# A fused transformer block: sums of four key tiles on GpSimd, and a last attention unit in which VectorE shares the adding and prepares the projection in pieces

## The chip, the cores and the metric

The kernel runs on one core of a Trainium2 chip. The metric is the time of one execution in device microseconds (us), the median over several runs. The core has five engines that run their own instruction streams and wait for each other by semaphores: TensorE (PE in the profile; PEld is its loading of weights), VectorE (DVE), ScalarE (ACT), GpSimd (POOL) and SyncE (SP), which here only issues DMAs. All arithmetic is in 32-bit floats.

## The reference, cut to what matters

The reference is a conditioned transformer block on x of shape (2, 2048, 512): two batches of 2048 tokens with 512 features.

```
mod = silu(cond) @ Wada + bada                     # six vectors of 512 for each batch
xm  = layernorm(x) * (1 + sc_a) + sh_a
q, k, v = xm @ Wqkv                                # 16 heads of 32 features
attn = softmax(where(causal, q k^T / sqrt(32), -inf))
x = x + gt_a * ((attn v) @ Wproj + bproj)          # "projection" below
xm = layernorm(x) * (1 + sc_m) + sh_m
x = x + gt_m * (gelu(xm @ W1 + b1) @ W2 + b2)      # the MLP, 2048 wide
```

The softmax needs, for each query and head, the sum over all keys of the exponentials. This row sum is what the change is about, together with the division by it.

## The kernel before, in words

The kernel goes through batch 0 (QKV, attention, projection), batch 1 (the same), and then the MLP for both.

**Units.** The 16 heads are taken in four groups `c` of four heads, since four heads of 32 features fill 128 partitions. The queries are taken in four blocks `i` of `QB` = 512. A pair (c, i) is a unit; there are 16 for each batch, in the order (0, 1, 2, 3) of `i` for c = 0 and (0, 2, 1, 3) for the others, so the last unit is (3, 3). The last four units' blocks are `last_order` = 0, 2, 1, 3, and the projection takes the blocks in this order.

**Steps.** A unit goes through the key tiles of 128 that a causal query block can see: `4 i` full tiles, and then three steps at the diagonal (the four partly masked tiles, two of which share a step). Unit (c, 3) has 12 full steps and 3 at the diagonal. In each step `scores_t` does for four heads: TensorE puts minus the row maximum into a PSUM bank (`st<-fold,sel`), adds the transposed scores (`st<-qst,kst`), and ScalarE takes the exponential into an SBUF tile (`e<-st`). At the diagonal GpSimd sets the masked part of `e` to zero (`affine_select`). There are four `st` banks and `E_BUFS` = 12 tiles `e`, three steps' worth.

**Maxima.** The row maximum of a unit has to be known before its steps. So while one unit is in its steps, TensorE computes score tiles of later units (`s<-kst,qst`, in PSUM banks of the pool `ps_s` or in borrowed `st` banks) and VectorE reduces them (`mx<-s`, or `junk<-s,causal` for the diagonal tiles). `due` spreads these tiles over the steps, by fixed costs, up to `AHEAD` = 2 units ahead. In the last unit nothing is left to do ahead.

**Values and row sums.** `LAG` = 2 steps later TensorE multiplies `e` by the values (`o<-e,vv`) and by ones, for the row sums (`sm<-…,ones`). Both have 32 output rows for each head. At the diagonal each step has its own row sums (`sm<-e,ones`). For the full key tiles GpSimd first adds the `e` of two steps (`pair_sums`, `ee<-e`, into one of `EE_BUFS` = 6 tiles), and one group of matmuls (`sm<-ee,ones`) serves the two. Work that comes later waits in a list `pending` with the step at which it is issued; `flush` issues it after that step's scores.

```
ee = pair_sums(even, es)                  # line 663
pending.append((now + LAG + 1,            # line 664
    lambda f=row_sums, ee=ee, first=n_step == 1: f(ee, first, False)))
```

**End of a unit.** `finish` copies `o` and `sm` to SBUF and writes them to HBM: attention outputs `od` and row sums `sd`. They are divided only at the projection. `inverses` loads the sums of a block as a [128, 64] tile `r`, VectorE takes the reciprocal, a DMA writes it to HBM (`rd`), and four DMAs, one for each `c`, read it back, each value broadcast over the 32 rows of its head, into a tile `rb` of 1 MB. Then VectorE multiplies the attention output by `rb`.

**The last unit and the projection.** At step 3 of the last unit `prefetch` (line 341) loads what the projection needs first, into the free key buffer `kst0`: Wproj, the outputs of the first two blocks (`at_s`), and x; it also takes the inverses of these two blocks and multiplies by them, as one VectorE operation of 128x2048 for each block (line 373). At step 7 `gate_weights` (line 375) brings the gate row into PSUM and multiplies bproj (`bgate`) and Wproj by it. `project_phase` (line 849) then takes 16 tiles of 128 tokens: GpSimd adds `bgate` to x (line 880), TensorE multiplies, VectorE adds the two, takes the statistics of the next layernorm and SP writes the row out. The inverses of the third and fourth blocks are taken there, in tiles n = 0 and n = 3, with their DMAs on ScalarE's queue (line 873). Between the tiles come the layernorm and transposes of the next stage.

**Order.** A scheduler orders instructions on each engine by its own model of the time, within what the data allow. Matmuls, the exponentials and the copies of `finish` are kept in program order (`mm`, `act`); other VectorE and GpSimd operations and the DMAs are placed by the scheduler. So VectorE's products with `rb` may be placed earlier or later than where they are written. All matmuls have line 190 in the profile, since one helper issues them.

Of the kernel before, what the change touches and what calls it, by code (L numbers as in the profile page):

```python
# [8 lines left out]
F32 = mybir.dt.float32  # L9
# [18 lines left out]
def dit_block_kernel(  # L28
# [31 lines left out]

    nc = tc.nc
    B, T, D = x.shape
    HID = W1.shape[1]
# [7 lines left out]
    NG = T // MT  # L73
    LAG = 2
    E_BUFS = 12
    EE_BUFS = 6
    AHEAD = 2

    const = ctx.enter_context(tc.tile_pool(name="const", bufs=1))
# [192 lines left out]
    class Row:  # L272
# [31 lines left out]
        def load_queries(self, u):  # L304
# [8 lines left out]
                )  # L313
            self.qst[u] = t

        def inverses(self, i, rb, queue):

            sums, inv = [
                d[self.b][i].rearrange("c h (p q) -> (c h p) q", p=P // (C * HC))
                for d in (sd, rd)
            ]
# [15 lines left out]
        def prefetch(self):  # L341

            st = bp.tile([P, HC, T], F32R, tag="kst0", name="kst")
            st = st.bitcast(F32).rearrange("p h t -> p (h t)")
            self.at_s = [  # L350
                st[:, n * C * QB : (n + 1) * C * QB].rearrange("p (c q) -> p c q", c=C)
                for n in range(2)
            ]
            self.xt_s = [st[:, (2 * C + n) * QB : (2 * C + n + 1) * QB] for n in range(TQ)]
            self.wproj = st[:, 3 * C * QB :].rearrange("p (c d) -> p c d", c=C)
            t = self.old_queries()
            self.next_s = [t[:, n, :] for n in range(TQ)]
# [12 lines left out]
            for k in range(2):  # L370
                rb = self.old_queries()
                self.inverses(last_order[k], rb, nc.sync)
                nc.vector.tensor_tensor(self.at_s[k], self.at_s[k], rb, ALU.mult)
# [107 lines left out]
    def attention_phase(row):  # L481
        b, vv, kst, qst = row.b, row.vv, row.kst, row.qst
        with pool(f"att{b}") as ap, pool(
# [4 lines left out]
            def scores_t(u, step, n):  # L488

                def st_bank():
                    return ps_stp.tile([P, QB], F32, tag="st", name="st")

                c, i = units[u]  # L500
                tiles = steps_of[u][step]
                q0 = tiles[0][1]
                w = sum(QB - q for _, q in tiles)
                sts, es = [], []
                row.score(max(0, n - 5))
                n = min(n, 5)
                for h in range(HC):
                    g = slice(h * HD, (h + 1) * HD)
                    st = st_bank()
                    mm(  # L510
                        st[:, :w], sel[g, :], fold[u % 2][g, q0 : q0 + w],
                        start=True, stop=False,
                    )
                    sts.append(st)
                for h in range(HC):
                    at = 0
                    for j, q in tiles:
                        mm(
                            sts[h][:, at : at + QB - q],
                            kst[c][:, h, j * P : (j + 1) * P],  # L520
                            qst[u][:, h, q:],
                            start=False, stop=at + QB - q == w,
                        )
                        at += QB - q
                    e = ap.tile([P, QB], F32, tag="e", name="e", bufs=E_BUFS)
                    act(nc.scalar.activation(e[:, :w], sts[h][:, :w], AF.Exp))  # L526
                    if tiles[0][0] >= i * TQ:

                        d = e.rearrange("p (t k) -> p t k", k=P)[:, 0 : TQ : TQ - 1, :]
                        d = d[:, : len(tiles), :]  # L530
                        nc.gpsimd.affine_select(  # L531
                            d, d, pattern=[[0, len(tiles)], [1, P]],
                            compare_op=ALU.is_ge, fill=0.0,
                            base=0, channel_multiplier=-1,
                        )
# [9 lines left out]
                    for _ in range(HC)  # L545
                ]

            def pair_sums(es0, es1):
                out = new_sums()
                for h in range(HC):  # L550
                    nc.gpsimd.tensor_tensor(out[h], es0[h], es1[h], ALU.add)  # L551
# [51 lines left out]
            for u, (c, i) in enumerate(units):  # L603
# [5 lines left out]
                for n_step, tiles in enumerate(steps_of[u]):  # L609
                    last = n_step == steps - 1  # L610
                    if n_step == 0:
                        o = ps_op.tile([P, QB], F32, tag="o", name="o")
                        sm = ps_op.tile([P, QB], F32, tag="sm", name="sm")
                    ready = row.at
# [5 lines left out]
                    if u + 1 < len(units) and row.rows_made == u + 1:  # L620
                        if last:
                            row.score(row.count(cum[-1], u + 1))
                        make_rows = last or (ready > u + 1 and n_step >= 1)
                    if u == len(units) - 1 and n_step == 3:
                        row.prefetch()
                    if u == len(units) - 1 and n_step == 7:
                        row.gate_weights()
                    flush(now)
                    if make_rows:
                        row.rows(u + 1)  # L630
# [14 lines left out]
                            es, tiles, first, last,  # L645
                        )

                    def row_sums(es, first, last, tiles=((0, 0),), sm=sm):
                        tile_by_tile(sm, lambda j, h: ones[:, :HD], es, tiles, first, last)

                    pending.append((now + LAG, values))
                    if n_step >= i * TQ:
                        pending.append(
                            (
                                now + LAG,
                                lambda f=row_sums, es=es, tiles=tiles, first=n_step == 0,
                                last=last: f(es, first, last, tiles),
                            )
                        )
# [189 lines left out]
    def project_phase(row, psum, between):  # L849
# [5 lines left out]
        with pool(f"proj{b}") as pp:  # L855
# [3 lines left out]
            for k, i in enumerate(last_order):  # L859
# [6 lines left out]
                for t in range(TQ):  # L866
                    if n in (0, TQ - 1):
                        d = 2 + n // (TQ - 1)
                        rbs[d] = (
                            row.old_queries() if d == 2  # L870
                            else pp.tile([P, C, QB], F32, tag="rb", name="rb")
                        )
                        row.inverses(last_order[d], rbs[d], nc.scalar)
                    nt = b * NT + i * TQ + t
                    if k == 0:
# [501 lines left out]
```

## Time and profile before

| | |
|---|---|
| median of 3 runs | 2572.67 us (2571.6 to 2576.87) |
| the profiled execution: own time, and span of its instructions | 2566.7 us, 2564.6 us |
| granted TensorE clock, mean | 0.989 |
| busy: TensorE, VectorE, ScalarE, GpSimd | 2502.6, 1301.8, 895.4, 845.1 us |
| attention of batch 0 and of batch 1 | 225 to 826 us, 1086 to 1687 us |
| unit 14 and last unit of batch 0 | 735.5 to 770.2 us, 770.2 to 826.5 us |
| projection of batch 0 and of batch 1 | 826.5 to 890.2 us, 1687.1 to 1753.5 us |

The profile gives for each engine the time in which it was busy. Matmuls are pipelined and overlap, so on TensorE the distance from one group's start to the next group's start is a better price than a duration. Idle time of an engine that nothing waits for costs nothing. In the lists of instructions the form is "output<-inputs", by the names of the tiles.

### The profile page before, as it was taken

The numbers are of one execution on the slowest core, as the hardware profiler recorded it, in microseconds if no ns is written. First come the engines' busy times: TensorE is split into PE (matmuls) and PEld (weight loads), VectorE is DVE, ScalarE is ACT, GpSimd is POOL, SyncE is SP. The second block draws the span as 40 slices with busy tenths as digits, with TensorE's granted clock in tenths as the row PEclk, the third lists the DMA queues.
The fourth block names the chain that finished last, engine by engine and source line by source line (L and its number), as shares of the span: only waits on it lengthen the run. The fifth ranks groups of instructions, "written<-read, shape, count | busy, mean of one in ns | idle before, by whom it ended". The sixth has DMA issues, their size and how long they took to land.

```text
span 2564.6 us, 31548 instructions
## 1 busy us (share of the span) xinstructions
PE 2502.6 (98%) x11361; PEld 1185.5 (46%) x11361; DVE 1301.8 (51%) x2732; ACT 895.4 (35%) x1667; POOL 845.1 (33%) x1038
## 2 busy tenths in 40 slices
PE   7999999999999999999999999899999999999998
PEld 3445445445443444454454445344444444444443
DVE  3455657666551635556665756245353344334424
ACT  1213455455545011254545454513312312311310
POOL 0001454544556366245545554632101100100100
PEclk9999999999999999999999999999999999999999
DMA  6645123041211798640414112144233332322422
GB/s 219 207 125 146 38 56 77 22 108 42 92 49 50 238 294 284 203 95 22 108 42 102 34 40 81 64 160 143 76 99 106 107 107 90 129 89 76 138 82 94
DMA packets 131718, 277.87 MB, mean 108 GB/s; under 512 B 13109, under 2 KB 41821, under 8 KB 127466
## 3 DMA queue, kind: packets, MB, share of 16 engines
q1 hardware_dynamic: 122818, 248.29, 32.7%
q0 software_dynamic: 5376, 23.07, 2.6%
q10 hardware_dynamic: 3368, 4.50, 0.5%
q8 instruction: 89, 1.46, 0.2%
q14 instruction: 67, 0.55, 0.1%
HBM read 201.90 MB, written 73.92 MB: 108 GB/s over the span
## 4 chain that ended last, share of the span: by engine, by line
PE 91%; DMA 4%; DVE 2%; issue 1%; POOL 1%; ACT 1%; SPq 0%; ACTq 0%; DVEq 0%; POOLq 0%
PE st L190 20%; PE ps_y L190 15%; PE ps_h L190 15%; PE o L190 10%; PE s L190 9%; PE ps_qk L190 8%; PE sm L190 6%; PE ps_v L190 4%; PE ps_o L190 2%; DMA rb<-r 1%; PE ps_xt L198 1%; DMA qst<-r 1%; DVE mx L407 1%; POOL ee L551 1%; PE ps_o L198 0%
## 5 line engine op out<-in xcount | busy, mean ns | idle before, releaser
L526 ACT ACTIVATE e<-st 128x512 f32<-128x512 f32 (+1 forms) x1152 | 575.5, 576 | 556.7 <-PE st L190 511.1
L551 POOL TENSOR_TENSOR ee<-e 128x512 f32<-128x512 f32 x384 | 489.3, 1305 | 423.1 <-ACT e L526 271.5
L407 DVE TENSOR_REDUCE mx<-s 128x1 f32<-128x512 f32 x616 | 413.8, 687 | 285.4 <-PE s L190 284.2
L190 PE MATMUL s<-kst,qst 128*128 128x512 f32 (+3 forms) x1058 | 451.3, 446 | 15.7 <-DVE mx L407 12.9
L190 PE MATMUL st<-qst,kst 128*128 128x512 f32 (+3 forms) x1280 | 435.4, 389 | 0.0
L190 PE MATMUL o<-e,vv 128*32 128x512 f32 (+3 forms) x2560 | 295.2, 542 | 0.0
L402 DVE CUSTOM_DVE_ANT_0 junk<-s,causal 128x384 bf16<-128x384 f32 (+3 forms) x442 | 211.3, 478 | 148.8 <-PE s L190 139.5
L190 PE MATMUL ps_h<-sx,w 128*128 128x512 f32 x640 | 286.7, 592 | 0.0
L190 PE MATMUL ps_y<-sh,w 128*128 128x512 f32 x640 | 277.8, 594 | 0.0
L190 PEld LDWEIGHTS st<-qst,kst 128*128 128x128 f32 x1280 | 227.8, 190 | 87.2 <-issue 62.8
L190 PEld LDWEIGHTS s<-kst,qst 128*128 128x128 f32 x1058 | 198.8, 189 | 140.5 <-DVE mx L407 57.5
L531 POOL TENSOR_SCALAR_AFFINE_SELECT e<-e 128x128 f32<-128x128 f32 (+1 forms) x384 | 124.9, 333 | 395.6 <-ACT e L526 389.2
L1148 POOL TENSOR_TENSOR c<-c 128x512 f32<-128x512 f32 x32 | 40.8, 1274 | 615.7 <-DVE c L1110 606.3
L190 PE MATMUL ps_qk<-xmT,wqkv 128*128 128x512 f32 x512 | 240.6, 598 | 2.2 <-DVE xmT L246 2.2
L1110 DVE TENSOR_TENSOR h<-c,ps_h 128x512 f32<-128x512 f32 x128 | 88.1, 688 | 231.4 <-PE ps_h L190 231.4
L190 PEld LDWEIGHTS ps_h<-sx,w 128*128 128x128 f32 x640 | 121.1, 190 | 150.2 <-issue 149.7
L190 PEld LDWEIGHTS ps_y<-sh,w 128*128 128x128 f32 x640 | 121.3, 191 | 148.5 <-issue 147.1
L190 PE MATMUL st<-fold,sel 32*128 32x512 f32 (+1 forms) x1152 | 162.4, 484 | 6.2 <-ACT e L526 3.8
L1134 ACT ACTIVATE h<-h,cols 128x512 f32<-128x512 f32 x128 | 92.4, 722 | 181.6 <-DVE h L1110 181.6
L190 PEld LDWEIGHTS st<-fold,sel 32*128 32x128 f32 x1152 | 64.6, 183 | 191.7 <-ACT e L526 110.0
L190 PEld LDWEIGHTS ps_qk<-xmT,wqkv 128*128 128x128 f32 x512 | 94.7, 191 | 97.6 <-issue 90.3
L190 PE MATMUL ps_v<-wqkv,xmT 128*128 128x512 f32 x256 | 122.8, 595 | 2.1 <-ACT xmT L251 2.1
(122 smaller groups left out, 2261.6 us busy)
## 6 DMA issues: line engine op xcount, KB each, us to landing
qst<-q SPq DMA_DIRECT2D x128, 256.0 KB
w<-w1d SPq DMA_DIRECT2D x34, 896.0 KB
w<-w2d SPq DMA_DIRECT2D x28, 1024.0 KB
kst<-k SPq DMA_DIRECT2D x24, 1024.0 KB
q<-hl SPq DMA_DIRECT2D x32, 512.0 KB
k<-hl SPq DMA_DIRECT2D x32, 512.0 KB
kst<-k SPq DMA_DIRECT2D x32, 256.0 KB
o<-ot SPq DMA_DIRECT2D x32, 256.0 KB
```

The lines of the kernel that those rows point to most:

```text
L190: return tc.keep_in_program_order(nc.tensor.matmul(*args, **kw))
L198: return tc.keep_in_program_order(nc.tensor.transpose(dst, src, ident[:n, :n]))
L402: nc.vector.tensor_tensor_reduce(junk[:, :w], s[:, :w], causal[:, QB - w :], 1.0, MASKED, ALU.add, ALU.max, m,)
L407: nc.vector.tensor_reduce(m, s[:, :w], axis=AX.X, op=ALU.max)
L526: act(nc.scalar.activation(e[:, :w], sts[h][:, :w], AF.Exp))
L531: nc.gpsimd.affine_select(d, d, pattern=[[0, len(tiles)], [1, P]], compare_op=ALU.is_ge, fill=0.0, base=0, channel_multiplier=-1,)
L551: nc.gpsimd.tensor_tensor(out[h], es0[h], es1[h], ALU.add)
L1110: nc.vector.tensor_tensor(dst, x, y, op)
L1134: nc.scalar.activation(d, d, AF.Gelu, bias=col(r_b1 + chunk, 1))
L1148: nc.gpsimd.tensor_tensor(c1_, c1_, c2_, ALU.subtract)
```

## The change

- **Sums of four.** The sums of two pairs are added into one (`four_sums`, in place in the first pair's `ee`), and one group of row-sum matmuls serves four key tiles. The addition is issued in the step after the second pair; its matmuls are issued `LAG + 2` steps after it. For the last four tiles before the diagonal the addition is made in two portions, heads 0 and 1 in one step and heads 2 and 3 in the next, so that the masks of a step don't queue behind four additions; its matmuls come one step later still. `EE_BUFS` goes from 6 to 12.
- **VectorE in the last unit.** In the last unit of a batch the additions of heads 1 and 3 are made by VectorE.
- **Preparing in pieces.** `prepare` takes the place of lines 624 to 627. `prefetch` at step 3 only loads, now the row sums of three blocks. At step 5 VectorE takes three reciprocals and multiplies `bgate` by the gate row; Wproj is multiplied in quarters in steps 5 to 8; at step 7 the inverses of two blocks are broadcast; the outputs are multiplied by them in quarters in steps 9 to 12. The third block's reciprocal is so taken in the last unit, and only its broadcast is left to the projection.
- **Order.** These VectorE operations, all additions and the masks are kept in program order.

```diff
-    EE_BUFS = 6
+    EE_BUFS = 12
...
+        def load_sums(self, i, queue):
+
+            r = bp.tile([P, C * HC * QB // P], F32, tag="r", name="r", bufs=3)
+            queue.dma_start(
+                r, sd[self.b][i].rearrange("c h (p q) -> (c h p) q", p=P // (C * HC))
+            )
+            return r
+
+        def invert(self, i, r, queue):
+            act(nc.vector.reciprocal(r, r))
+            queue.dma_start(
+                rd[self.b][i].rearrange("c h (p q) -> (c h p) q", p=P // (C * HC)), r
+            )
+
         def inverses(self, i, rb, queue):
...
-            r = bp.tile([P, C * HC * QB // P], F32, tag="r", name="r", bufs=2)
-            queue.dma_start(r, sums)
-            nc.vector.reciprocal(r, r)
-            queue.dma_start(inv, r)
             for c in range(C):
...
-            for k in range(2):
-                rb = self.old_queries()
-                self.inverses(last_order[k], rb, nc.sync)
-                nc.vector.tensor_tensor(self.at_s[k], self.at_s[k], rb, ALU.mult)
-
-        def gate_weights(self):
-
-            ps = rows_of(ps_sp, 0, self.b, "s")
-            nc.vector.tensor_tensor(bgate, bgate, ps, ALU.mult)
-            for c in range(C):
-                nc.vector.tensor_tensor(
-                    self.wproj[:, c, :], self.wproj[:, c, :], ps, ALU.mult
-                )
+            self.r_s = [self.load_sums(i, nc.sync) for i in last_order[:3]]
+
+        def prepare(self, n):
+
+            if n == 3:
+                self.prefetch()
+            elif n == 5:
+                for k in range(3):
+                    self.invert(last_order[k], self.r_s[k], nc.sync)
+                self.ps_gate = rows_of(ps_sp, 0, self.b, "s")
+                act(nc.vector.tensor_tensor(bgate, bgate, self.ps_gate, ALU.mult))
+            elif n == 7:
+                self.rb_s = [self.old_queries() for _ in range(2)]
+                for k in range(2):
+                    self.inverses(last_order[k], self.rb_s[k], nc.sync)
+            if 5 <= n < 5 + C:
+                w = self.wproj[:, n - 5, :]
+                act(nc.vector.tensor_tensor(w, w, self.ps_gate, ALU.mult))
+            elif 9 <= n < 9 + C:
+                for k in range(2):
+                    d, r = self.at_s[k][:, n - 9, :], self.rb_s[k][:, n - 9, :]
+                    act(nc.vector.tensor_tensor(d, d, r, ALU.mult))
...
-            def pair_sums(es0, es1):
+            def add(u, h, dst, x, y):
+                vector = u == len(units) - 1 and h % 2
+                act((nc.vector if vector else nc.gpsimd).tensor_tensor(dst, x, y, ALU.add))
+
+            def pair_sums(u, es0, es1):
                 out = new_sums()
                 for h in range(HC):
-                    nc.gpsimd.tensor_tensor(out[h], es0[h], es1[h], ALU.add)
+                    add(u, h, out[h], es0[h], es1[h])
                 return out
+
+            def four_sums(u, ee0, ee1, heads):
+                for h in heads:
+                    add(u, h, ee0[h], ee0[h], ee1[h])
...
-                    if u == len(units) - 1 and n_step == 3:
-                        row.prefetch()
-                    if u == len(units) - 1 and n_step == 7:
-                        row.gate_weights()
+                    if u == len(units) - 1:
+                        row.prepare(n_step)
                     flush(now)
...
+                    if later:
+                        four_sums(u, *later.pop(0))
 
                     pending.append((now + LAG, values))
...
-                        ee = pair_sums(even, es)
-                        pending.append(
-                            (
-                                now + LAG + 1,
-                                lambda f=row_sums, ee=ee, first=n_step == 1: f(
-                                    ee, first, False
-                                ),
+                        ee = pair_sums(u, even, es)
+                        if n_step % 4 == 1:
+                            ee0 = ee
+                        else:
+
+                            end = n_step + 1 == i * TQ
+                            for heads in ([(0, 1), (2, 3)] if end else [range(HC)]):
+                                later.append((ee0, ee, heads))
+                            pending.append(
+                                (
+                                    now + LAG + 2 + end,
+                                    lambda f=row_sums, ee=ee0: f(ee, False),
+                                )
                             )
-                        )
...
+                        if d == 3:
+                            row.invert(
+                                last_order[d],
+                                row.load_sums(last_order[d], nc.scalar),
+                                nc.scalar,
+                            )
                         row.inverses(last_order[d], rbs[d], nc.scalar)
```

More of the change, by code (lines that the diff above doesn't have):

```diff
@@ L314, in load_queries @@
             self.qst[u] = t
-        def inverses(self, i, rb, queue):
[L322 to L325, printed above, removed]
-            r = bp.tile([P, C * HC * QB // P], F32, tag="r", name="r", bufs=2)
-            queue.dma_start(r, sums)
-            nc.vector.reciprocal(r, r)
-            queue.dma_start(inv, r)
+        def load_sums(self, i, queue):
[9 more added lines that the diff above has]
+            )
+        def inverses(self, i, rb, queue):
             for c in range(C):
@@ L530, in scores_t @@
                         d = d[:, : len(tiles), :]
[L531 to L534, printed above, removed]
+                        act(
+                            nc.gpsimd.affine_select(
+                                d, d, pattern=[[0, len(tiles)], [1, P]],
+                                compare_op=ALU.is_ge, fill=0.0,
+                                base=0, channel_multiplier=-1,
+                            )
                         )
@@ L611, in attention_phase @@
                     if n_step == 0:
+                        summed, later = set(), []
                         o = ps_op.tile([P, QB], F32, tag="o", name="o")
@@ L646, in values, with row_sums @@
                         )
-                    def row_sums(es, first, last, tiles=((0, 0),), sm=sm):
+                    def row_sums(es, last, tiles=((0, 0),), sm=sm, summed=summed):
+                        first = not summed
+                        summed.add(len(summed))
                         tile_by_tile(sm, lambda j, h: ones[:, :HD], es, tiles, first, last)
+                    if later:
+                        four_sums(u, *later.pop(0))
                     pending.append((now + LAG, values))
@@ L655, in attention_phase @@
                                 now + LAG,
-                                lambda f=row_sums, es=es, tiles=tiles, first=n_step == 0,
-                                last=last: f(es, first, last, tiles),
+                                lambda f=row_sums, es=es, tiles=tiles, last=last: f(
+                                    es, last, tiles
+                                ),
                             )
@@ L872, in project_phase @@
                         )
+                        if d == 3:
[3 more added lines that the diff above has]
+                                nc.scalar,
+                            )
                         row.inverses(last_order[d], rbs[d], nc.scalar)
```

## The prediction

> **What bounds the kernel now.** I read the page first: busy shares, the chain that ended last, the groups.
>
> ```profile
> PE 2502.6 (98%) x11361; PEld 1185.5 (46%) x11361; DVE 1301.8 (51%) x2732; ACT 895.4 (35%) x1667; POOL 845.1 (33%) x1038
> ...
> PE 91%; DMA 4%; DVE 2%; issue 1%; POOL 1%; ACT 1%; SPq 0%; ACTq 0%; DVEq 0%; POOLq 0%
> ...
> L551 POOL TENSOR_TENSOR ee<-e 128x512 f32<-128x512 f32 x384 | 489.3, 1305 | 423.1 <-ACT e L526 271.5 <-PE sm L190 151.6
> ```
>
> TensorE is the bound: 98% busy, 91% of the chain. Time is saved by taking matmuls from it or by closing its few idle stretches. GpSimd adds pairs of `e` tiles 384 times and is idle two thirds of the span, for lack of `e` (271.5 us) or of a free `ee` buffer (151.6).
>
> Then the timeline of TensorE in batch 0's last unit, where no score tile is left:
>
> ```profile
> 782.41 1.09 PE L190 MATMUL st<-fold,sel 32*128 32x512 f32 x4
> 783.43 1.20 PE L190 MATMUL st<-qst,kst 128*128 128x512 f32 x4
> 784.56 1.06 PE L190 MATMUL sm<-ee,ones 128*32 128x512 f32 x8
> 785.45 1.04 PE L190 MATMUL o<-e,vv 128*32 128x512 f32 x8
> 786.42 0.50 PE L190 MATMUL st<-fold,sel 32*128 32x512 f32 x4
> 786.85 1.20 PE L190 MATMUL st<-qst,kst 128*128 128x512 f32 x4
> 787.98 1.07 PE L190 MATMUL o<-e,vv 128*32 128x512 f32 x8
> 788.98 1.09 PE L190 MATMUL st<-fold,sel 32*128 32x512 f32 x4
> ...
> 804.19 0.50 PE L190 MATMUL st<-fold,sel 32*128 32x512 f32 x1 [1.15 <-ACT e L526]
> ```
>
> Columns are start, duration, engine, line and operation; in brackets, idle time and who ended it. A step handles one key tile for four heads and runs from one group of four `fold` matmuls to the next. Matmuls overlap, so prices come from starts, not from durations: from `sm` to `o` it is 785.45 − 784.56, and 0.88 us over several such pairs. The starts also show a second limit. After a step with a row sum the folds take 0.43; after one without they take 1.01, as they wait for ScalarE to empty the `st` banks. The rest of a step is 1.13 for `st` and 1.0 for `o`; call this the fold rule. So without score tiles a pair (with, without) takes 4.00 + 2.56 = 6.57, two steps without 2 × 3.13 = 6.27: a removed row sum saves only 0.3 there. With score tiles (`s`, for later units) between, ScalarE has time: in unit (1,3) a step with four score tiles took 4.44 with a row sum and 3.58 without; with five, 4.60 and 3.71. There it saves all 0.88. At 804.19 `e` is late, since four `bgate` adds (5.0 us) stood before the `ee` adds on GpSimd; that step took 7.95.
>
> Last, the stall in unit 14:
>
> ```profile
> 742.07 6.98 POOL L551 TENSOR_TENSOR ee<-e 128x512 f32<-128x512 f32 x4 [8.64 <-ACT e L526]
> 745.62 2.31 DVE L373 TENSOR_TENSOR kst<-kst,qst 128x2048 f32<-128x2048 f32 x1 [5.80 <-DMA qst<-r]
> 747.85 1.27 DVE L407 TENSOR_REDUCE mx<-s 128x1 f32<-128x512 f32 x2
> 748.58 0.79 PE L190 MATMUL s<-kst,qst 128*128 128x512 f32 x1 [5.94 <-DVE mx L407]
> ```
>
> VectorE waits for the broadcast inverses to multiply the first old block by them; the maxima that free the score banks queue behind it, and TensorE waits 5.9 us, after which the clock is granted at half for some microseconds (0.89 on average over 740 to 770). That step took 11.41, its like in unit 10 3.97. Batch 1 shows 11.41 too.
>
> [...] the four adds at 742.07 took 6.98 where four elsewhere take 5.0, with a VectorE product of 2.31 inside. [...] here 1.255 us undisturbed, against 0.69 for VectorE's 512. [...] The broadcasts of `r` have 4; their DMA share was 0.24, and 1 MB took 12.7 us from issue to landing.
>
> **Row sums.** 96 groups of `sm<-ee` (four heads, 8 matmuls each) become 48; at 0.88 that is at most 42.2. The plan of score tiles per step is unchanged. They come later: quads ending at steps 3 and 7 are summed at steps 7 and 11, a unit's last one in step 1 of the next unit.
> - i=1 units of c 0 to 2, scores throughout: 6 × 0.88 = 5.3.
> - i=2 units: 8 × 2 × 0.88 = 14.1.
> - i=3 units of c 0 to 2: steps 4, 6, 8, 10 lose 3.5; step 7 and step 1 of the next gain 1.76; the tail without scores goes +1.02, −1.44, +0.58, −0.4 by the fold rule. Net −2.0 each, six of them: 12.
> - i=1 of c=3, its tail without scores: 1.2 × 2 = 2.4.
> Sum 33.8.
>
> **GpSimd.** It gains 192 adds, less what VectorE takes. Per quad 12 × 1.255 = 15.1, while four steps in an i=3 unit become about 15.7. `e` has three steps of buffers: from the steps, `e` of step 11 is needed from 44.8 us after the unit's start, and the adds of step 9 that free its buffers run 41.2 to 45. The masks of step 12 end at 51.2, its values start at 54.3; two portions at the diagonal keep the next masks (55.6) ahead of theirs (60). No stall, but little slack. [...]
>
> **Unit 14.** Reciprocals and products leave it, so its step 1 falls from 11.41 to about 4.0, −7.4 in each batch: 14.8. What is late next is the maxima themselves, at the normal pace.
>
> **The last unit.** Before 56.3. By the fold rule, with row sums in steps 1, 7, 11 and at the end and the one matmul group of the gate row (1.05) in step 5, the steps are 3.42, 3.43, 2.56, 3.14, 3.13, 4.18, 2.56, 4.0, 2.56, 3.13, 3.13, 4.0, 2.56, 3.3 and 6.72: 51.8. The long step of 7.95 is gone, since two heads' adds leave GpSimd and the four `bgate` adds stand between pairs. VectorE has no maxima here (busy 7.2 of 56.3 us), so its 18 adds and 8 products of 0.69 are covered, unless it waits. New waits:
> - [...] I get those adds done 38 to 40 us in, where `e` of step 11 wants its buffer from 36.7. About 2; between 0 and 5.
> - VectorE's products of steps 9 to 12 wait in order for 8 broadcast DMAs on one 4-engine path: the reciprocals run at about 15.2 to 16.9 us into the unit, the broadcasts are issued from 17.6, the first four have landed at 30, the others follow every 2.5 until 40. Behind the products queue the odd heads' adds of steps 9 and 11, whose `e` is ready at 32 and 39, and behind those ScalarE's next `e`: within the 2 above.
> - ScalarE's queue holds the third block's broadcasts after step 11; the first waits for VectorE's last product with the old buffer, so the exponentials of step 12 wait about 1.5 (0 to 5).
> - `prepare` moves three loads of `r` (0.4 each), three stores (0.3) and 8 broadcasts (0.6 each) down SP's queue; only unit 15's stores are behind: nothing.
> 55.3, so −1 each: −2. Without any of these waits it is −4.5 each, −9 for both.
>
> **Projection.** Before 63.7 and 66.4, against 16 tiles × 3.48 (the first six took 20.87) = 56 plus transposes. In batch 0 `rstd` now precedes the broadcasts on ScalarE, which freed VectorE only at 845.9; but the fourth block's reciprocal moves behind about 7 us of work. I take −1 (−5 to +4). In batch 1 the reciprocal moves from after the first tile to after the third, 4.6 later, and VectorE waited 13 us in all for those four broadcasts: +4 (0 to +7). Sum +3.
>
> **Total.** −33.8 − 14.8 − 2 + 3 = −47.6: the profiled span 2564.6 becomes 2517, its own 2566.7 becomes 2519. The median of the runs, 2572.67, lies 6 above that one; 2525 on its scale.
>
> **Rivals.**
> 1. *ScalarE takes the gain.* If 0.3 holds everywhere, row sums give 14: about 2544. For: the folds' 1.01. Against: 4.44 to 3.58 with scores. Chance 0.17.
> 2. *The waits move to the end.* The 4-engine broadcasts land 5 later under load, ScalarE and VectorE stand behind them in both last units (+10), and batch 1's projection takes its 7: about 2538. For: VectorE's four waits in batch 1's projection. Against: the last unit's DMA share is 0.09. Chance 0.16.
> 3. *GpSimd becomes the bound.* 34 quads outside the last units have 15.7 us each. An add must cost 1.42 to eat 48 us; at 1.5, 34 × 2.3 = 78 gives about 2603, slower. For: the mean is 1.305[...]. Against: 1.255 undisturbed. Chance 0.06, most of it slower.
> 4. *Fewer sums are not issued.* The changed order has 192 head sums for 384, so 0.01.
>
> The forecast has 0.60. Faster than 0.2% (5 us, about what a measurement of this kernel tells from no change) 0.93, same 0.02, slower 0.05. Range 2508 to 2548: below, every row sum outside the last units at its full price (42 × 0.88 = 37), the last units at −9 and the projection at −5 in batch 0 and 0 in batch 1, 66 in all; above, rivals 1 and 2 at their prices, and some us for both in part. Left out are rival 3 and the ends of both.
>
> **What would show it.** Right: `sm<-ee` 384 matmuls for 768; scored steps without it near 3.6; unit 14's second step near 4 to 5; GpSimd's `ee` mean under 1.35; no wait of ScalarE for `ee` above 1 in units 0 to 14. Wrong: `e` waiting for `ee` throughout (rival 3), folds at 1.0 in scored steps (rival 1), `kst<-kst,qst` waiting for `qst<-r` above 5 with `e` behind it (rival 2).

## The result, and the profile after

The kernel after took **2542.4 us** (median of 4 runs, 2540.48 to 2547.66), the kernel before 2572.14 beside it (2570.12 to 2576.87): a ratio of 0.9886, with a 95% interval of 0.9868 to 0.9903. So it is faster by 30 us, and 17 above the forecast of 2525. The profiled execution took 2543.34, its span is 2541.5.

The page of the kernel after (busy shares, the chain of work that ended last, two groups of instructions):

```profile
PE 2472.5 (97%) x10977; PEld 1182.4 (47%) x10977; DVE 1359.0 (53%) x2780; ACT 894.8 (35%) x1667; POOL 1034.5 (41%) x1194
...
PE 90%; DVE 5%; DMA 4%; issue 1%; ACT 1%; POOL 0%; ACTq 0%; SPq 0%; DVEq 0%; POOLq 0%
...
L564 POOL TENSOR_TENSOR ee<-e 128x512 f32<-128x512 f32 x360 | 458.9, 1308 | 257.6 <-ACT e L538 256.9
...
L564 POOL TENSOR_TENSOR ee<-ee 128x512 f32<-128x512 f32 x180 | 229.6, 1303 | 0.0
```

TensorE has 384 matmuls less and is still the bound. GpSimd's additions cost 1.31 us each and fit: GpSimd is in no part of the chain worth a percent. But VectorE has gone from 2% to 5% of the chain. By stages, from the starts of TensorE's groups in the two profiled executions (us):

| stage | before | after | forecast | measured |
|---|---|---|---|---|
| QKV of batch 0 | 225.1 | 226.1 | 0 | +1.0 |
| units 0 to 14, batch 0 | 545.1 | 524.4 | −24.3 | −20.7 |
| last unit, batch 0 | 56.3 | 60.4 | −1 | +4.1 |
| projection, batch 0 | 63.6 | 64.5 | −1 | +0.9 |
| QKV of batch 1 | 196.4 | 199.9 | 0 | +3.5 |
| units 0 to 14, batch 1 | 544.1 | 522.4 | −24.3 | −21.7 |
| last unit, batch 1 | 56.6 | 60.2 | −1 | +3.6 |
| projection, batch 1 | 66.2 | 70.5 | +4 | +4.3 |
| MLP, to the last group's start | 806.1 | 807.8 | 0 | +1.7 |

The sum is −23.3 where −47.6 was forecast. The profiled execution of before lay some 5 to 6 below its median, that of after 1 above, so the medians differ by more: 29.7.

**Unit 14** is as forecast. TensorE's waits in it, in batch 0 of the kernel after (columns: who waited for whom, total, times, longest):

```profile
PE ps_m L199 <- DVE mhl L434: 0.4, 1, 0.4
```

The wait of 5.9 is gone, and step 1 takes 4.84 with a row sum in it, where it took 11.41.

**The last unit** follows the fold rule through step 11 to within 0.02 in every step (3.43, 3.42, 2.56, 3.13, 3.13, 4.18, 2.56, 3.99, 2.55, 3.14, 3.14, 4.00). Then step 12 takes 7.48 for 2.56, step 13 6.38 for 3.3. The timelines of ScalarE and of TensorE there:

```profile
790.62 0.60 ACT L538 ACTIVATE e<-st 128x512 f32<-128x512 f32 x1 [0.60 <-DVE ee L564]
795.84 0.62 ACTq L334 DMA_DIRECT2D qst<-r  x1
796.56 0.60 ACT L538 ACTIVATE e<-st 128x512 f32<-128x512 f32 x1 [5.35 <-DVE kst L394]
```

```profile
792.82 1.06 PE L191 MATMUL o<-e,vv 128*32 128x512 f32 x8
797.21 2.26 PE L191 MATMUL st<-fold,sel 32*128 32x512 f32 x4 [3.33 <-ACT e L538]
799.40 2.40 PE L191 MATMUL st<-qst,kst 128*128 128x384 f32 x8
```

ScalarE has a DMA at the head of its queue, the third block's first broadcast. It writes into a tile that VectorE's last product (`kst<-kst,qst`, L394) still reads. The four exponentials of step 12 stand behind it for 5.35 us, and TensorE waits 3.33 for them. The folds and `st` matmuls after the wait take 2.26 and 2.40, for 1.09 in the step from 785.73 and 1.36 in the same step of the kernel before. The windows of TensorE's granted clock (the column before the last two) show it lower there:

```profile
790.60:797.20 6.60, 2.62 (x13) 1.01 (x13) 6.60 (x10) 1.24 (x3) 1.04 (x1) 0.89 0.10 40
797.20:804.60 7.40, 7.39 (x26) 4.22 (x27) 0.41 (x1) 3.62 (x7) 5.41 (x10) 0.50 0.27 94
804.60:810.90 6.30, 6.30 (x76) 2.51 (x75) 1.29 (x2) 1.40 (x5) 1.12 (x4) 0.89 0.15 59
```

The clock is 0.50 for the 7.4 us after the wait; the 0.89 of the windows on both sides adds, by an estimate from these shares, some 1.4 us at half each, so the lower clock lasts about 10 us. In this trace it follows TensorE's wait of 3.33; the last section has cases in which it came without such a wait.

VectorE is late with this product. Its timeline and GpSimd's show two delays just before:

```profile
782.46 1.76 DVE L394 TENSOR_TENSOR kst<-kst,qst 128x512 f32<-128x512 f32 x1
786.19 0.95 DVE L394 TENSOR_TENSOR kst<-kst,qst 128x512 f32<-128x512 f32 x1 [1.98 <-DMA qst<-r]
787.07 3.46 DVE L564 TENSOR_TENSOR ee<-e 128x512 f32<-128x512 f32 x2
```

```profile
785.32 6.33 POOL L564 TENSOR_TENSOR ee<-e 128x512 f32<-128x512 f32 x4
```

A product waits 1.98 for its broadcast. And two additions take 3.46, 1.73 each instead of 0.69, with GpSimd's at 1.58 instead of 1.26. Record by record the ends alternate: GpSimd's at 786.59, 788.29 and 789.98, VectorE's 0.54 to 0.55 after each. So each of the two engines is slower while the other works.

**Step 4 of the units (1, 1) and (2, 1)** is the other place. It has six score tiles and takes 6.02, 6.23, 6.04 and 6.01 us (before: 4.89 with a row sum of 0.88). Timelines of GpSimd, VectorE and TensorE in unit (2, 1) of batch 0 of the kernel after, and VectorE's two small operations in the same step of the kernel before:

```profile
590.87 5.01 POOL L564 TENSOR_TENSOR ee<-e 128x512 f32<-128x512 f32 x4 [3.64 <-ACT e L538]
```

```profile
593.65 1.01 DVE L433 CAST mhl<-m 128x16 fp32r<-128x16 f32 x1
594.70 1.21 DVE L434 TENSOR_TENSOR mhl<-m,mhl 128x16 fp32r<-128x16 f32 x1
595.83 0.41 DVE L414 CUSTOM_DVE_ANT_0 junk<-s,causal 128x256 bf16<-128x256 f32 x1
```

```profile
596.30 0.33 PE L191 MATMUL s<-kst,qst 128*128 128x128 f32 x1 [0.67 <-DVE mx L414]
```

```profile
601.20 0.17 DVE L421 CAST mhl<-m 128x16 fp32r<-128x16 f32 x1
601.40 0.18 DVE L422 TENSOR_TENSOR mhl<-m,mhl 128x16 fp32r<-128x16 f32 x1
```

`split` ends a unit's maxima with a copy and a subtraction of 16 elements in each partition. They take 1.01 and 1.21 us while GpSimd adds, and 0.17 and 0.18 in the kernel before, where GpSimd is idle at that moment. Four additions in 5.01 us end about every 1.25, and each of the two ends just after one of them. Behind them queue the maxima that free the score banks.

### The profile page after: what moved, and what is told of

The parts are those of the page before. It is cut to its first block, busy times and chain, and to the rows that moved or that the text cites. A ratio compares the mean times of both kernels' runs of the same rounds, so it can differ in the third digit from the quotient of the medians.

```text
span 2541.5 us, 30886 instructions
## 1 busy us (share of the span) xinstructions
PE 2472.5 (97%) x10977; PEld 1182.4 (47%) x10977; DVE 1359.0 (53%) x2780; ACT 894.8 (35%) x1667; POOL 1034.5 (41%) x1194
## 4 chain that ended last, share of the span: by engine, by line
PE 90%; DVE 5%; DMA 4%; issue 1%; ACT 1%; POOL 0%; ACTq 0%; SPq 0%; DVEq 0%; POOLq 0%
PE st L191 19%; PE ps_y L191 15%; PE ps_h L191 15%; PE o L191 10%; PE s L191 9%; PE ps_qk L191 8%; PE sm L191 4%; PE ps_v L191 4%; PE ps_o L191 3%; DVE junk L414 1%; DMA qst<-r 1%; PE ps_xt L199 1%; DMA rb<-r 1%; DVE mx L419 1%; DMA k<-hl 1%
## 5 line engine op out<-in xcount | busy, mean ns | idle before, releaser
L564 POOL TENSOR_TENSOR ee<-e 128x512 f32<-128x512 f32 x360 | 458.9, 1308 | 257.6 <-ACT e L538 256.9
L191 PEld LDWEIGHTS st<-qst,kst 128*128 128x128 f32 x1280 | 232.1, 194 | 87.6 <-issue 63.6
L564 POOL TENSOR_TENSOR ee<-ee 128x512 f32<-128x512 f32 x180 | 229.6, 1303 | 0.0
L191 PE MATMUL st<-fold,sel 32*128 32x512 f32 (+1 forms) x1152 | 166.7, 487 | 10.7 <-ACT e L538 8.3
```

The lines of the kernel that those rows point to most:

```text
L191: return tc.keep_in_program_order(nc.tensor.matmul(*args, **kw))
L564: act((nc.vector if vector else nc.gpsimd).tensor_tensor(dst, x, y, ALU.add))
```

## Experiments

All times are medians beside runs of the kernel before in the same session (2569.8 to 2572.9).

**Third block's broadcasts on SP's queue**

```diff
-                        row.inverses(last_order[d], rbs[d], nc.scalar)
+                        row.inverses(
+                            last_order[d], rbs[d], nc.sync if d == 2 else nc.scalar
+                        )
```

> After with the four broadcasts of the third block on SP's queue. Theory Q (the stall at the end of the last unit is ScalarE's own queue: the first of these DMAs holds the exponentials of step 12 until VectorE's last product has released the tile; the half clock that follows is a consequence): ScalarE's wait of 5.35 us before step 12 falls below 1.5, step 12 goes from 7.48 to 3.5 to 4.5, and the last unit from 60.5 and 60.2 to 55 to 56.5; 8 to 11 us in all. Theory P (VectorE and GpSimd are late with the sums themselves, [...] and free the exponentials' tiles too late): the wait stays above 3 us, now ended by an addition, and the unit stays above 59.

2539.67 us (ratio 0.9879, 0.9861 to 0.9898). The last units fell from 60.4 and 60.2 to 53.3 and 54.8, more than theory Q said; step 12 took 4.09 and 5.54. In the first of them ScalarE waited for VectorE only this much:

```profile
ACT e L538 <- DVE ee L564: 1.6, 2, 1.0
```

So the stall and the half clock after it were ScalarE's queue (the unit is 7.1 shorter, for a wait of TensorE of 3.33); theory P falls as the cause of the stall. Yet the whole gained only 2.7, for 8 to 11 expected and within the spread of the runs. In batch 0 the 7.1 us were given back: projection 68.0 (+3.5), QKV of batch 1 204.1 (+4.2). In batch 1 the 5.4 were too: units 0 to 14 526.4 (+4.0, of which 2.5 is a step at half the clock, see the last section), projection 73.1 (+2.6). One part is the edit's own, since the last unit's stores now follow the broadcasts on SP's queue. ScalarE's wait for the stored sums in the projection was 2.35 in the kernel after; here:

```profile
808.07 1.28 ACT L207 ACT_TABLE_LOAD   x1 [5.65 <-DMA s<-sums]
```

**`split` on GpSimd**

```diff
-            nc.vector.tensor_copy(hl[:, :, :, 0], m)
-            nc.vector.tensor_tensor(
+            nc.gpsimd.tensor_copy(hl[:, :, :, 0], m)
+            nc.gpsimd.tensor_tensor(
```

> After with the copy and the subtraction that end a unit's maxima (`split`, 128x16 elements each) on GpSimd instead of VectorE. Theory L (step 4 of the i = 1 units of c = 1 and 2 takes 6.0 to 6.2 us because these two small VectorE operations are locked out by four row-sum additions of GpSimd, and the maxima queue behind them): these four steps go to 3.9 to 4.3, about 8 us less in all, and VectorE's wait in front of maxima goes. Rival R (the step has six score tiles and VectorE's maxima are simply the limit there): 5.8 or more stays. Rival W (GpSimd's additions now queue behind the two, which wait for the maxima): ScalarE waits for `ee` in the i = 3 units, and the time rises.

2536.31 us (0.9868, 0.9853 to 0.9883). The four steps took 4.52, 4.53, 4.52 and 4.57: 6.2 us less in all, theory L. They stop at 4.5 and not at 4.0; in unit (2, 1) of batch 0 TensorE still waits 0.19 there for a maximum, and what the rest is stays open. GpSimd does the two in 0.4 us ahead of its additions:

```profile
590.44 0.20 POOL L433 CAST mhl<-m 128x16 fp32r<-128x16 f32 x1 [6.42 <-DVE m L431]
590.72 0.22 POOL L434 TENSOR_TENSOR mhl<-m,mhl 128x16 fp32r<-128x16 f32 x1
590.89 5.00 POOL L564 TENSOR_TENSOR ee<-e 128x512 f32<-128x512 f32 x4
```

Rival W had the direction of one effect: in units 0 to 14 of batch 0 ScalarE's waits for additions grew from 6.7 to 12.4 us (longest 2.7). But the (c, 3) units take the same 56.5 to 56.8 us, so this cost nothing.

**Sums of two on GpSimd in the last unit**, first with the broadcasts on ScalarE's queue, then on SP's

```diff
-                vector = u == len(units) - 1 and h % 2
+                vector = False
...
                         ee = pair_sums(u, even, es)
-                        if n_step % 4 == 1:
+                        if u == len(units) - 1:
+                            pending.append(
+                                (now + LAG + 1, lambda f=row_sums, ee=ee: f(ee, False))
+                            )
+                        elif n_step % 4 == 1:
```

Theory P is here that the eighteen additions make VectorE late.

> After, with only the last unit of each batch changed: sums of two key tiles there, all on GpSimd (24 additions of 1.26 us = 30 us in a unit of over 50), VectorE keeps the preparation alone. By the fold rule three more row-sum groups cost 0.9 us in all, so 52.7 without waits. Theory P [...]: VectorE's last product comes about when the broadcasts land, step 12 starts without a long wait, and the unit takes 53 to 55.5; 10 to 14 us less in all. Theory Q alone (the queue of ScalarE waits for broadcasts that land late whatever VectorE does): ScalarE's wait at step 12 stays near 5 and the unit at 59 to 61.

2553.52 us (0.9936, 0.9923 to 0.9949), last units 65.3 and 64.8: neither theory. The scheduler, which places this DMA by its own clock, had put it in front of step 8's exponentials:

```profile
790.65 1.19 ACTq L334 DMA_DIRECT2D qst<-r  x2
791.94 0.60 ACT L538 ACTIVATE e<-st 128x512 f32<-128x512 f32 x1 [12.35 <-DVE kst L394]
```

The same mechanism, 12.35 us for 5.35. It says nothing on VectorE's share. The same with SP's queue:

> The kernel with sums of two on GpSimd in the last unit once more, now with the third block's broadcasts on SP's queue, so that no exponential can stand behind them wherever the scheduler puts them. Theory Q (ScalarE's queue was the whole stall, in after as in the kernel with sums of two): no wait of ScalarE above 2 in the last unit, 52.5 to 54 us, within 1.5 of the kernel with sums of four and broadcasts on SP's queue (53.3 and 54.8), since three more row-sum groups cost 0.9 by the fold rule. Theory P (the additions shared with VectorE cost time by themselves): 3 us or more below it.

2541.04 us (0.9885, 0.9858 to 0.9911), last units 58.9 and 59.1: 5 above the higher of the two theories. No exponential stands behind a DMA now, but step 10 takes 10.27. GpSimd's timeline:

```profile
774.51 5.93 POOL L924 TENSOR_TENSOR kst<-kst,bgate 128x512 f32<-128x512 f32 x4 [0.98 <-DVE bgate L383]
780.41 12.58 POOL L564 TENSOR_TENSOR ee<-e 128x512 f32<-128x512 f32 x8
```

The four `bgate` additions stand before eight row-sum additions, as they stood before four in the kernel before (7.95 there). In the kernel after, where VectorE takes half of the additions, there is no such step; the next run keeps sums of four and takes VectorE's half away.

**All additions of the last unit on GpSimd, sums of four, broadcasts on SP's queue** (`vector = False`)

> After with all additions of the last unit on GpSimd (sums of four) and the third block's broadcasts on SP's queue: what VectorE's share of the adding is worth. GpSimd then has 36 additions of 1.26 us (45 us), four of bgate (6 us) and 4 us of masks in a unit of 53[...]: it becomes the limit, exponentials wait for `ee`, and the last unit takes 58 to 63. Rival: GpSimd's slack was enough, and it stays at 53 to 55; then sharing buys nothing.

2554.82 us (0.9939, 0.992 to 0.9959), last units 64.2 both. ScalarE waited 10.4 us for `ee` in the first, and steps 9 and 10 there took 5.87 and 9.62: the long step is back. Against 53.3 and 54.8 with the same queue, VectorE's share is worth about 10 us in each batch, although the two engines slow each other (1.73 and 1.58 us an addition in the kernel after).

**Sums of four alone**: the preparation of the kernel before, and `vector = False`

> Sums of four alone, all additions on GpSimd, with the preparation of the kernel before. The row sums outside the last units bring their 33.8 us of the forecast less the 8 us of the four long steps; unit 14 keeps its stall (step 1 near 11.4). In the last unit GpSimd has 36 additions (45 us) and four of bgate (5 us)[...]: it becomes the limit there, and the unit grows from 56.3 to 58 to 64. Sum against before: 26 less, 4 to 15 more: 11 to 22 us faster. If additivity holds, this and the preparation alone add up to more than the whole change brought.

2561.39 us (0.9961, 0.9945 to 0.9978): 10 us faster, just below the expected 11. Step 1 of unit 14 took 14.32, not 11.4 (VectorE waits 6.4 for a broadcast), and the last units 61.4. So the row sums alone give back some 14 us: 2 in each unit 14 (14.32 against 11.41 + 0.88) and 5 in each last unit. The other two parts of the change, which keep this from happening, bring 19 of the 30 us.

**Fourth block's inverses at the projection's first tile**

```diff
-                    if n in (0, TQ - 1):
-                        d = 2 + n // (TQ - 1)
+                    for d in (2, 3) if n == 0 else ():
```

> After with the fourth block's row sums, reciprocal and broadcasts written at the first tile of the projection instead of the fourth. Theory R (the projection of batch 1 grew by 4.1 us because the change keeps this reciprocal in order behind the products of the third block; it ran 12.6 us into the projection instead of 6.7): the reciprocal comes 6 to 8 us in, TensorE's wait of 9.5 for the transposes falls to 3 to 5, the projection of batch 1 goes from 70.5 to 65 to 67 and that of batch 0 from 64.5 to 61 to 64; 5 us in all, nothing elsewhere. Rival D (the broadcasts land when four DMA engines and the 3 MB of Wqkv let them, whenever they are issued): both stay within 1 us.

2535.99 us (0.987, 0.984 to 0.99). The projection of batch 1 went from 70.5 to 66.9, that of batch 0 to 64.2. VectorE's reciprocal and the first product behind it, first in the kernel after (projection from 1657.9), then in this one (from 1655.1):

```profile
1670.51 0.52 DVE L326 RECIPROCAL r<-r 128x64 f32<-128x64 f32 x1
1681.25 0.69 DVE L930 TENSOR_TENSOR at<-at,rb 128x512 f32<-128x512 f32 x1 [4.23 <-DMA rb<-r]
```

```profile
1661.76 0.55 DVE L326 RECIPROCAL r<-r 128x64 f32<-128x64 f32 x1 [0.71 <-DMA r<-s]
...
1673.53 0.69 DVE L929 TENSOR_TENSOR at<-at,rb 128x512 f32<-128x512 f32 x1 [5.41 <-DMA rb<-r]
```

Theory R in batch 1: the reciprocal comes 6.7 us into the projection instead of 12.6, the first product with `rb` 18.4 instead of 23.4. In batch 0 theory D was nearer. VectorE's waits for `rb` hardly shrank (12.5 for 14.2): all comes earlier, but no faster.

**SP's queue, `split` on GpSimd and early inverses together**

> After with three edits together: third block's broadcasts on SP's queue, `split` on GpSimd, the fourth block's inverses early. If the three causes are separate and right, 12 us in the last units (less what the projection gives back, 3 us in each batch when the fourth block is late, which the early reciprocal should take away), 6 in the four long steps and 5 in the projections: 2542 becomes 2516 to 2523. If gains ahead of the projection are eaten by a broadcast that lands at a fixed time, 2526 to 2533.

2529.1 us (0.9839, 0.9815 to 0.9864): the second of the two cases. The last units took 53.3 both, the four steps 4.5 to 4.6, but batch 0's projection 69.6 and the QKV after it 205.1. Early inverses did not buy back what SP's queue costs.

**Wide broadcasts**

```diff
-            for c in range(C):
+            for h in range(HC):
                 queue.dma_start(
-                    rb[:, c, :],
-                    rd[self.b][i][c].unsqueeze(1).to_broadcast([HC, HD, QB]),
+                    rb[h * HD : (h + 1) * HD],
+                    rd[self.b][i][:, h, :].unsqueeze(0).to_broadcast([HD, C, QB]),
                 )
```

> After with each broadcast cut by head instead of by c: four DMAs of 256 KB for a block as before, but each now repeats a 4x512 source over 32 partitions as its outermost dimension, where it was 4 heads outermost. Theory F (the broadcasts are slow because they run on 4 of 16 engines, and the waits in the projection are waits for them): the four for the fourth block land about 3 us after their issue instead of 7 to 20, VectorE's waits for rb (10.5 and 14.2 us) fall below 4, TensorE's wait of 9.5 in batch 1's projection falls to 0 to 5, and the projections from 64.5 and 70.5 to 59 to 62 and 62 to 66; the last unit loses the 2.0 us wait of a product, and its stall becomes shorter: 54 to 59. In all 10 to 20 us. Rival D (what limits them is the number of 2 KB rows, or the reading of one place again and again): the same waits within 2 us.

**2514.77 us** (0.9776, 0.9756 to 0.9796), 28 less than the kernel after: beyond the expectation. The busy share of the 16 DMA engines in tenths and GB/s, in 40 slices of 0.6 us, in the last unit of batch 0, in which the eight broadcasts run; first the kernel after (768 to 792), then this one (770 to 794):

```profile
DMA  0000430122222322222222222222222222222222
GB/s 0 0 0 3 92 69 0 41 89 102 102 102 102 130 102 102 102 102 102 102 99 102 102 102 99 102 102 102 102 102 102 102 102 102 102 102 102 102 102 102
```

```profile
DMA  0000222459998788999999731000000000000000
GB/s 0 0 0 0 55 55 55 157 181 328 249 236 178 164 171 195 266 253 205 212 253 201 160 72 44 0 0 0 0 0 0 0 0 0 0 0 0 0 0 0
```

Narrow, they run flat at 102 GB/s with a share of 0.2 to 0.3 and are not done when the window ends; wide, at about 200 GB/s with a share near 0.9, done in some 10 us. The records of single packets say the same. Both have 1024 packets of 2 KB; from the first to the last it takes 21.1 us narrow and 10.7 wide. Narrow, 4 of them are under way for 83% of the time from 778 to 790; wide, up to some 18 are. So the narrow ones keep about 4 of 16 engines busy (a share of 0.23 is 3.7 engines), and rival D falls, since the number and size of the rows are unchanged. What the edit changed is the source's outermost dimension, which was 4 and is 32. The projections fell to 58.4 and 59.1. In batch 1 the only DMA that VectorE waits for there is no broadcast:

```profile
DVE at L930 <- DMA at<-o: 1.0, 1, 1.0
```

The last units fell to 54.4 both. There part may be the scheduler's, which put the third block's first DMA one step later in ScalarE's queue. With `split` on GpSimd and early inverses added:

> The wide broadcasts, `split` on GpSimd and the fourth block's inverses early, with the third block's broadcasts still on ScalarE's queue. If the causes are separate: the gain of the wide broadcasts alone, 6 more in the four long steps, 2 to 4 more in the projections: 2512 to 2524, and below the three edits with SP's queue (2529.1), where the third block's broadcasts held up the stores of the last unit's outputs. If the first of the third block's broadcasts still holds the exponentials of step 12, the last unit stays above 58 and the time is 2522 to 2532.

2510.1 us (0.9753, 0.9732 to 0.9774), below the 2512 to 2524 expected: four steps 4.5 to 4.9, last units 54.4. And with the eight products block by block (`k = (n - 9) // 2`, two quarters of one block in each step):

> As the kernel before it, and the eight products of the last unit go block by block (steps 9 and 10 the first, 11 and 12 the second), so that the tile which the third block's broadcasts reuse is free one to two steps earlier. If ScalarE's stall is its wait for this tile, it goes wholly and the last unit takes 52 to 54: 4 to 12 us less than without this edit. If the stall had gone already, no difference above 2 us.

2513.2 us (0.9765, 0.9751 to 0.9779), last units 57.2 and 55.5: no gain, and neither of the two outcomes expected. In batch 0 the scheduler had put the first DMA in front of step 12's exponentials again, which waited 2.80 us for VectorE, and the long step is the last, 9.75 us, with the clock at 0.56 from 797.2 to 800.5. The intervals of the three wide versions overlap, so which is best is not settled; all three beat the kernel after and before.

**Wide broadcasts in the kernel before** (same edit)

> The kernel before, with its broadcasts cut by head as in the wide version of after (2514.8). It asks how much of the 27 us that wide broadcasts brought to after belongs to the change's own new waits, and how much the kernel before had to give as well. Theory A (most of it is the change's: its products and ScalarE's queue stood behind narrow broadcasts in the last unit): here only the 5.8 us wait of VectorE in each unit 14 and the rb waits of the projections shrink; step 1 of unit 14 from 11.41 to 6.5 to 8.5, the projections from 63.6 and 66.2 to 58.5 to 61, the last units unchanged at 56 to 57; 14 to 20 us, so 2552 to 2558, and the change is worth 37 to 43 us on top, 7 to 13 more than between the two narrow kernels. Rival B (wide broadcasts bring both kernels the same): 2543 to 2547.

2552.89 us (0.9924, 0.9905 to 0.9943), 17 less. Step 1 of unit 14 fell to 3.97 (more than expected; step 3 rose from 3.79 to 5.06), the projections to 57.2 and 59.1, the last units rose to 59 (step 10, the one of 7.95, took 10.7), and QKV of batch 1 to 205.1. With wide broadcasts on both sides the change is worth 38 us (2552.89 − 2514.77), against 30 with narrow ones: theory A.

## Why the prediction was right, and where its sum was off

- **Bound and sign.** TensorE stayed the bound and the likeliest case held. The forecast of 2525 was 17 too low, inside its range: by the medians the gain is 30 of 48 us, in the profiled executions 23, half of what was forecast. Rival 3 (GpSimd) fell: 1.308 us an addition. Rival 4 fell.
- **Row sums.** Right. In the (c, 3) units the steps with score tiles that lost their row sum take 3.55 to 3.98, and took 4.42 to 4.82; rival 1 fell. The tails without score tiles came out 0.6 us shorter than forecast (steps 11 and 14 take 3.42 and 3.75, for 3.57 and 4.20). What was missed is step 4 of the (1, 1) and (2, 1) units: four times 2.0 against 4.0, **8 us**. What failed is the author's assumption that GpSimd's additions don't hold up VectorE's work on the scores: true of the maxima, which take 0.68 beside additions as without, not of the `split` between them (1.01 and 1.21 for 0.17 and 0.18). Moving it to GpSimd took 6.2 us of the 8 away. All else in units 0 to 14 gave 2 more than forecast, so units 0 to 14 miss by 6.2 in all.
- **GpSimd.** Room enough, though ScalarE waited up to 1.7 for an addition in units 0 to 14, where none above 1 was expected.
- **Unit 14.** −14.8 forecast; step 1 is 3.96 without its row sum, so −14.9.
- **Last unit.** Forecast 55.3, measured 60.4 and 60.2: **10 us** in the two. The mis-sized term is ScalarE's queue, "about 1.5 (0 to 5)": the wait was 5.35, and the half clock behind it was not priced at all, although unit 14 of the kernel before had shown one (0.50 from 748.5 to 752.0, after TensorE's wait of 5.94). Its three waits were also added as if independent. The timelines argue that they feed each other: adding beside GpSimd makes VectorE's additions late (1.73 each), the narrow broadcasts its products (a wait of 1.98), and both set when ScalarE's DMA gets its tile. The broadcasts were issued from 20.6 us into the unit, not from 17.6. Without the DMA on ScalarE's queue the unit takes 53.3 and 54.8, 1.5 and 3.0 above the 51.8 without waits, so for the adding side by side and the broadcasts alone the author's estimate of 2 was about right. Rival 2 had this mechanism, and its time of 2538 was nearer. The argument against it, a DMA share of 0.09, was a misreading: it is a mean over the whole last unit of the kernel before and over 16 engines, and while narrow broadcasts run it is 0.23, about 4 engines busy throughout.
- **Projection.** +4 for batch 1: 4.3, and the early reciprocal took 3.6 of it away. Batch 0: +0.9 for −1.
- **Untouched code**: 6.2 us in the profiled executions, forecast as nothing. In QKV of batch 1 the same code took 196.3 to 205.1 us over these kernels. ScalarE waits there for stores, for instance in the kernel with three edits together:

```profile
937.87 0.60 ACT L765 ACTIVATE hl<-ps_qk 128x512 fp32r<-128x512 f32 x1 [9.68 <-DMA k<-hl]
```

VectorE's half of the same work waits for ScalarE's (7.31 us there, to 938.50), and its maxima queue behind (TensorE waits 5.1 for maxima in the stage, in two waits). What decides the length is **open**; no run varied this stage.

## What to carry to other kernels

Before work is moved onto an engine, list what stands behind it in each queue, DMAs on a compute engine's queue included: here a DMA that waited for a tile held the exponentials behind it for 5.35 us, and TensorE's wait of 3.33 us was followed by two steps 3.7 us longer than the fold rule, the first of them at a clock of 0.50. When a DMA share is flat, here at 0.23, ask whether the transfer can use more engines before taking it for a path with room; here the shape of the destination and source was worth nearly as much as the whole change. And look for small operations between the large ones: here two of 16 elements, with inputs in SBUF, took 1.01 and 1.21 us beside GpSimd's additions, for 0.17 and 0.18 without, where the maxima of 512 elements, with inputs in PSUM, took 0.68 either way.

## What was not expected of the hardware

- Issuing eight narrow broadcasts one after the other took SP 11.9 us: 0.5 to 0.7 each for the first four, 1.8 to 2.4 for the others, issued while the first were in flight. Eight wide ones took 3.67 (in the kernel with `split` on GpSimd and early inverses too).
- VectorE and GpSimd adding side by side slow each other down: 1.73 and 1.58 us an addition instead of 0.69 and 1.26. Sharing still won 10 us in the last unit.
- With `split` on VectorE and sums of four, step 5 of unit (1, 1) took 6.4 to 6.6 instead of 3.9 to 4.2 in 6 of 16 passages; with `split` on GpSimd in none of 8. In exactly these 6 the granted clock is at half (0.52 over the 6.4 us of step 5 in batch 1 of the kernel with SP's queue), in the other 18 it is full (1.00 in both of the kernel after). Yet TensorE's waits in step 4 just before, 1.2 to 1.3 us in all and none above 0.7, are the same in the kernel after, where the clock stays up. So the half clock came here without a long wait; what decides is open.
